# A conv, state-space and attention block: the scan's input in a ring of three PSUM banks, the depthwise 3x3 on shifted copies, and TensorE work in smaller pieces

## The chip, the cores and the metric

The kernel runs on one core of a Trainium2 chip. The metric is the device time of the whole program in microseconds (us). Profiles are of one execution, taken by the hardware profiler. The engines are called PE (TensorE, matrix multiplication), PEld (its weight loads), DVE (VectorE), ACT (ScalarE), POOL (GpSimd) and SP (SyncE, which issues the DMAs). PSUM is the memory that PE writes, eight banks of 128 partitions x 512 float32 values.

## The reference

Input x has 8 images of 384 channels and 32 x 32 pixels (1024 positions). Layer 0 adds to x a selective state-space model, run forward and backward over the positions, and a gated depthwise convolution. Layer 1 is causal attention with 6 heads, then a feed-forward network with weights that are Kronecker products. All is float32.

```python
# layer 0, per direction; xn = rmsnorm(x) over channels
u, z = split(in_proj(xn))
u = silu(causal_conv4(u) + conv1d_b)
dt, Bm, Cm = split(x_proj(u))
delta = softplus(dt_proj(dt) + dt_proj_b)
deltaA = exp(delta[..., None] * A)
deltaBu = (delta * u)[..., None] * Bm[:, :, None, :]
h[t] = deltaA[t] * h[t-1] + deltaBu[t]       # 16 states for each of 384 channels
y = (sum_n h[n] * C[n] + u * D) * silu(z)
global_feat = out_proj(y)                    # forward + backward, times scale_mod
local_feat = sigmoid(depthwise3x3(xn) + dw_b) * xn
x = x + res_scale * (global_feat + local_feat)
# layer 1, on tokens
t = t + attention(layernorm(t))
t = t + gelu(layernorm(t) @ kron(c_fc_1, c_fc_2).T) @ kron(c_proj_1, c_proj_2).T
```

## The kernel before

**One list of operations, ordered by a planner.** The program first declares every operation (`op`, lines 105 to 153) with its engine, an assumed cost, what it reads and writes, and a due time `at`. `Plan.run` (155 to 264) then goes through an assumed clock: each engine in turn takes, of the operations that could start now, the one with the earliest due time. The outcome is one fixed order for each engine, and the engines meet only through semaphores. An operation here may hold several instructions, which then stand together on the engine; a projection, for instance, is one operation of three matmuls. The assumed costs (`pe`, `act`, `dve`, `pool`, 79 to 92) shape the order only, they aren't waited for. A `Window` (407 to 424) spreads due times over a stretch, and `EVICT`, `SUMS`, `PRODUCTS`, `DECAY` (403) move due times of some kinds forward. `STAY` (98) is how long ACT prefers operations with the activation table that is loaded.

**Buffers** are slots of a kind (`kinds`, 379 to 383). The PSUM banks are divided into five for general use (`psm`), one pair for the scan's input (`b`), and one for the scan's output sums (`y`). Most tiles in the other memory share 26 slots (`t`).

**The scan** (`scans` 841, `group` 905). A group is 8 channels x 16 states on 128 partitions, over 1024 positions; there are 96 groups per image (48 in each direction), 768 in all. A group takes these steps: a DMA broadcasts delta to `dA`, with six slots (914); ACT makes exp(delta*A) of it (919); PE spreads delta*u to the 16 states with two matmuls, one per half of the positions, into `b` (926 to 931); DVE multiplies `b` by B, in place (932); DVE scans, reading `dA` and `b` (935); POOL multiplies by C (938); PE sums over the states into `y`, on four groups of 32 columns (875 to 884). The matmul for a group is declared to come as early as it can, but `b` has one slot, so it waits until the scan of the group before has read it.

**Around it** run, for other images, `project` (613, input projection), `gates` (681), `prepare` (692, the convolution of 4 taps, as four column groups on shifted copies, then `products` and `delta`), `local` (741, the depthwise 3x3 and its gate), `finish` (941) and `layer1` (1019, attention and the feed-forward network). `local` multiplies, for every block of 128 channels and half, nine diagonal 128 x 128 matrices by shifted views of the padded image `xm`, in three operations of three matmuls. `delta` (795) makes two matmuls of 24 rows, one for each half, in turn. In `project_in` DVE adds the bias of v when it takes v from PSUM (1062).

Matmuls all have line 311 in the profile, since a helper issues them; a row is told apart by its tiles (`pw` is the depthwise bank, `b` the scan's input, `s` the scores, `t` the transposes). A float32 matmul of the program is two instructions in the profile. DMAs all have line 391.

Of the kernel before, what the change touches and what calls it, by code (L numbers as in the profile page):

```python
# [9 lines left out]
F32 = mybir.dt.float32  # L10
# [7 lines left out]
P = 128  # L18
# [12 lines left out]
TAPS = 4  # L31
KP = 4
# [58 lines left out]
def pe(n, k=1):  # L91
    return k * (0.04 + n * 0.0012)


class Plan:
    LATENCY = 0.15
    SWITCH = 1.3
    STAY = 7.0
# [169 lines left out]
def conv_attn_hybrid_kernel(  # L268
# [85 lines left out]
    nc.vector.tensor_reduce(by4, ident.rearrange("p (m k) -> p m k", k=TAPS), AX.X, ALU.max)  # L354
    eye8 = const.tile([P, GC], F32, name="eye8")
# [12 lines left out]
    for c in range(CT):  # L368
# [8 lines left out]

    TB = PADDED * 4
# [3 lines left out]
        "psm": (5, HALF * 4), "b": (1, L * 4), "y": (1, HALF * 4),  # L382
    }
    sb = ctx.enter_context(tc.tile_pool(name="sb", bufs=1))
    pp = ctx.enter_context(tc.tile_pool(name="pp", bufs=1, space=PSUM))
    plan = Plan({k: n for k, (n, _) in kinds.items()})
# [11 lines left out]

    EXP, SILU, GELU = "natural_log_exp_and_others", "silu_and_others", "gelu_and_others"
# [3 lines left out]
    EVICT, SUMS, PRODUCTS, DECAY = 0.0, 10.0, 10.0, 15.0  # L403

    PREPARE, PROJECT, LAYER1 = (0.05, 0.75), (0.7, 1.0), (1.1, 2.1)
# [39 lines left out]
    wld = [array([P, 9, P], f"wld_{c}") for c in range(CT)]  # L445
# [6 lines left out]
    w_dt = held([P, P], "w_dt")  # L452
# [3 lines left out]
    bvb = held([P, C], "bvb")  # L456
# [4 lines left out]
    def setup_early():  # L461
# [52 lines left out]
        for c in range(CT):  # L514
            dma(
                lambda c=c: w_dt.t[c * KI : c * KI + RANK, :], lambda c=c: dt_wT[:, c * P : (c + 1) * P], [], [(w_dt, c)], 0
            )
# [22 lines left out]
    def setup_late():  # L540
# [5 lines left out]
        for c in range(CT):  # L546
            wl = tl(f"wlm_{c}", [P, 9, P])
            for k in range(9):
                op(
                    "POOL", 0.4, lambda wl=wl, c=c, k=k: nc.gpsimd.tensor_scalar_mul(wl.t[:, k], ident, col("dw_w", c, k)),  # L550
                    [], [(wl, k)],
                )
            dma(lambda c=c: wld[c].t, lambda wl=wl: wl.t, [wl], [wld[c]], P * 9 * P * 4)
# [7 lines left out]
    def setup_layer1():  # L561
# [6 lines left out]
        dma(lambda: bvb.t, lambda: bv.partition_broadcast(P), [], [bvb], 0)  # L568
# [44 lines left out]
    def project(b):  # L613
# [21 lines left out]
        for hf in range(NH):  # L635
            p = bank(f"pss_{b}_{hf}")

            def total(p=p, hf=hf):
                for c in range(CT):
                    mm(p.t, ones, sq[c].t[:, half(hf)], c == 0, c == CT - 1)  # L640

            op("PE", pe(HALF, 3), total, sq, [p], holds=xp)
# [15 lines left out]
    def into(b, w, xp, win):  # L658
# [3 lines left out]
        for m in range(CT):  # L662
            t = tl(f"{'uz'[w]}t_{b}_{m}")
            for hf in range(NH):
                p = bank(f"pi_{b}_{w}_{m}_{hf}")

                def proj(p=p, m=m, hf=hf):
                    for c in range(CT):
                        mm(grid(p.t), win.t[:, c, chans(m)], inside(xp[c].t, hf), c == 0, c == CT - 1)

                op("PE", pe(HALF, 3), proj, [(v, hf) for v in xp] + [win], [p], holds=[t])
                op("ACT", act(HALF), lambda p=p, t=t, hf=hf: nc.scalar.copy(t.t[:, half(hf)], p.t), [p], [(t, hf)])  # L672
# [19 lines left out]
    def prepare(b):  # L692
# [5 lines left out]
        for c in range(CT):  # L698
# [11 lines left out]
            for hf in range(NH):  # L710
                for d in range(2):
# [9 lines left out]
                    op("PE", pe(HALF, 2.4), conv, ct + [wc], [p], holds=[u])  # L721
# [19 lines left out]
    def local(b):  # L741

        s = b % 2
        for c in range(CT):
            xr, xm, wl = tl(f"xr_{b}_{c}"), tl(f"xm_{b}_{c}", [P, PADDED]), tl(f"wl_{b}_{c}", [P, 9, P])
            dma(lambda t=wl: t.t, lambda c=c: wld[c].t, [wld[c]], [wl], P * 9 * P * 4)
            dma(lambda t=xm: t.t, lambda c=c: xpd[s].t[chans(c)], [(xpd[s], c)], [xm], P * PADDED * 4)
            dma(lambda t=xr: t.t, lambda c=c: x[b, chans(c)].rearrange("p h w -> p (h w)"), [], [xr], P * L * 4)
            for hf in range(NH):
                p = bank(f"pw_{b}_{c}_{hf}")  # L750

                for dy in range(3):

                    def conv(p=p, hf=hf, wl=wl, xm=xm, dy=dy):
                        xg = xm.t.rearrange("p (h w) -> p h w", w=WP)
                        for dx in range(3):
                            mm(
                                grid(p.t), wl.t[:, dy * 3 + dx], xg[:, dy + hf * RH : dy + (hf + 1) * RH, dx : dx + W],
                                dy + dx == 0, dy + dx == 4,
                            )  # L760

                    op("PE", pe(HALF, 3), conv, [xm, wl], [p], holds=[xr])
# [7 lines left out]
                def mix(p=p, hf=hf, xr=xr, xm=xm):  # L770
                    nc.vector.scalar_tensor_tensor(grid(p.t), grid(p.t), 1.0, inside(xm.t, hf), ALU.add, ALU.mult)
                    nc.vector.scalar_tensor_tensor(
                        xr.t[:, half(hf)], p.t, hres.t, xr.t[:, half(hf)], ALU.mult, ALU.add
                    )

                op("DVE", 2 * dve(HALF), mix, [xm, hres], [p, (xr, hf)])
            dma(lambda c=c: based[s].t[chans(c)], lambda t=xr: t.t, [xr], [(based[s], c)], P * L * 4)

    def products(b, d, us, wc):
# [3 lines left out]
        for hf in range(NH):  # L783
            p = bank(f"px_{b}_{d}_{hf}")

            def proj(p=p, hf=hf):
                for c in range(CT):
                    mm(p.t, wc.t[:, c, 0:P], us[d][c].t[:, half(hf)], c == 0, c == CT - 1)

            op("PE", pe(HALF, 3), proj, us[d] + [wc], [p], holds=[xd])  # L790
# [4 lines left out]
    def delta(b, d, c, du, xd):  # L795
# [6 lines left out]
        r = slice(c * KI, c * KI + RANK)  # L802
        for hf in range(NH):
            p = bank(f"pd_{n}_{hf}")
            op(
                "PE", pe(HALF), lambda p=p, hf=hf: mm(p.t, w_dt.t[r, :], xd.t[r, half(hf)]),
                [(xd, hf), (w_dt, c)], [p], holds=[e, de],
            )

            def split(p=p, hf=hf):  # L810
# [3 lines left out]
            op("ACT", 2 * act(HALF) + 0.1, split, [p], [(e, hf), (de, hf)])  # L814
# [565 lines left out]
```

## Time and profile before

| | us |
|---|---|
| median of 3 runs (lowest, highest) | 4458.82 (4454.85, 4462.86) |
| the profiled execution | 4449.86 |
| its span, first to last instruction | 4448.1 |
| first scan starts | 151.5 |
| last scan starts | 4185.0 |

The page cuts the span into 40 slices; each digit is the busy share of a slice in tenths. The scans run from slice 2 to slice 38, and no engine is at 9 throughout:

```profile
PE   5587777789897998989997898979989798888798
DVE  1566768888788788788788787888878788888622
ACT  4648554676667657676577666677567665556355
POOL 2957846896469855797559964698548974576322
DMA  6786795577876669566776678667795667456300
```

A group of instructions is read as line, engine, operation, what it writes and reads, their sizes and the count, then busy us and mean ns of one, then the engine's idle time just before such instructions and which instruction ended most of it. The next rows are of other operations that the change touches:

```profile
L1316 ACT ACT_TABLE_LOAD x234 | 300.2, 1283 | 4.2
L311 PE MATMUL pd<-xd,w_dt 24*128 24x512 f32 x192 | 115.8, 712 | 21.8 <-ACT de L812 18.7 <-ACT p L1108 2.1 <-DVE xr L772 0.8
L1064 DVE TENSOR_TENSOR v<-pvv,bvb 128x512 f32<-128x512 f32 x48 | 32.6, 680 | 66.6 <-PE pvv L311 66.6
```

### The profile page before, as it was taken

What the parts mean: (1) busy time and instruction counts of PE and PEld (TensorE: products, weight loads), DVE (VectorE), ACT (ScalarE), POOL (GpSimd) and SP (SyncE); (2) the same over time, 40 slices, a digit from 0 to 9 for tenths busy, and PEclk for the clock granted to TensorE, in tenths of its full rate; (3) what the DMA queues carried; (4) which work ended last, traced back from release to release, by engine and by line L of the source; (5) the groups of instructions that cost most, each with busy time, mean ns of one, the idle gap of its engine ahead of it and who ended that gap; (6) DMA issues with size and microseconds to landing.
All of it is one profiled execution on the core that took longest, in us unless ns stands there. A gap on an engine that the chain in (4) does not pass through costs nothing. (4 is left out here: it accounts for less than half of the span.)

```text
span 4448.1 us, 52858 instructions
## 1 busy us (share of the span) xinstructions
PE 3800.7 (85%) x17682; PEld 1558.8 (35%) x17682; DVE 3341.6 (75%) x2940; ACT 2799.7 (63%) x4524; POOL 3010.2 (68%) x2385
## 2 busy tenths in 40 slices
PE   5587777789897998989997898979989798888798
PEld 2132222334233442433323342334424343343254
DVE  1566768888788788788788787888878788888622
ACT  4648554676667657676577666677567665556355
POOL 2957846896469855797559964698548974576322
PEclk7697787799998999889998999989998899999799
DMA  6786795577876669566776678667795667456300
GB/s 212 232 272 201 229 270 165 163 226 204 220 200 178 209 185 274 159 199 207 222 220 179 206 212 220 203 180 208 212 255 163 202 182 205 136 146 181 98 6 34
DMA packets 297068, 853.55 MB, mean 192 GB/s; under 512 B 33812, under 2 KB 87132, under 8 KB 296796
## 3 DMA queue, kind: packets, MB, share of 16 engines
q1 hardware_dynamic: 296796, 850.18, 66.3%
q8 instruction: 140, 2.29, 0.2%
q14 instruction: 132, 1.08, 0.1%
HBM read 677.25 MB, written 174.59 MB: 192 GB/s over the span
## 5 line engine op out<-in xcount | busy, mean ns | idle before, releaser
L938 POOL TENSOR_TENSOR h<-h,bc 128x1024 f32<-128x1024 f32 x768 | 1811.9, 2363 | 1047.6 <-DVE h L935 745.6
L935 DVE TENSOR_TENSOR_SCAN h<-dA,b 128x1024 f32<-128x1024 f32 x768 | 1755.5, 2286 | 96.7 <-ACT dA L919 19.7
L932 DVE TENSOR_TENSOR b<-b,bc 128x1024 f32<-128x1024 f32 x768 | 943.8, 1229 | 652.5 <-PE b L311 532.3
L919 ACT ACTIVATE dA<-dA,nA 128x1024 f32<-128x1024 f32 x768 | 870.2, 1147 | 338.4 <-DMA dA<-ded 317.2
L311 PE MATMUL b<-du,dup 32*128 32x512 bf16 x1536 | 328.4, 421 | 403.3 <-DVE h L935 356.6
L311 PE MATMUL y<-h,sel 128*32 128x512 f32 x3072 | 599.5, 690 | 46.1 <-POOL h L938 45.0
L311 PE MATMUL pw<-xm,wl 128*128 128x512 f32 x864 | 413.8, 619 | 7.8 <-ACT de L812 4.2
L1108 ACT ACTIVATE p<-s,mx 128x512 f32<-128x512 f32 (+3 forms) x576 | 328.9, 580 | 123.6 <-DVE mx L1102 120.7
L311 PEld LDWEIGHTS <-dup 32*128 32x128 bf16 x1536 | 75.5, 92 | 909.0 <-DVE h L935 597.4
L1153 POOL TENSOR_SCALAR p<-p,den 128x512 f32<-128x512 f32 (+3 forms) x576 | 329.3, 592 | 80.3 <-DVE den L1146 79.0
L1167 ACT COPY pT<-t 128x512 f32<-128x512 f32 (+3 forms) x576 | 253.8, 486 | 176.2 <-PE t L1160 169.4
L1160 PE MATMUL t<-ident,p 128*128 128x128 f32 x1728 | 297.2, 311 | 77.3 <-POOL p L1153 54.9
L1102 DVE TENSOR_REDUCE mx<-s 128x1 f32<-128x512 f32 (+3 forms) x576 | 286.3, 545 | 70.2 <-PE s L311 63.5
L1316 ACT ACT_TABLE_LOAD x234 | 300.2, 1283 | 4.2
L1160 PEld LDWEIGHTS t<-ident,p 128*128 128x128 f32 x1728 | 216.2, 157 | 223.8 <-POOL p L1153 129.8
L311 PE MATMUL s<-k,q 64*128 64x512 f32 (+3 forms) x1152 | 286.2, 565 | 4.6 <-ACT p L1108 3.4
L311 PE MATMUL pi<-xp,win 128*128 128x512 f32 x576 | 274.6, 618 | 11.9 <-ACT zt L672 10.4
L311 PE MATMUL pc<-pT,v 128*64 128x128 f32 x3456 | 248.8, 292 | 5.6 <-ACT pT L1167 5.6
L311 PEld LDWEIGHTS pc<-pT,v 128*64 128x64 f32 x3456 | 201.3, 145 | 89.0 <-issue 45.0
L311 PEld LDWEIGHTS pw<-xm,wl 128*128 128x128 f32 x864 | 158.2, 195 | 195.7 <-issue 184.5
L838 POOL TENSOR_TENSOR u<-u,part 128x1024 f32<-128x1024 f32 x96 | 205.3, 2138 | 18.0 <-ACT part L830 18.0
L830 ACT CAST part<-u 128x1024 bf16<-128x1024 f32 x144 | 150.5, 1045 | 94.3 <-POOL u L838 51.6
(169 smaller groups left out, 4766.1 us busy)
## 6 DMA issues: line engine op xcount, KB each, us to landing
dA<-ded SPq DMA_DIRECT2D x768, 512.0 KB
ct<-urd SPq DMA_DIRECT2D x96, 513.5 KB
du<-dusd SPq DMA_DIRECT2D x96, 512.0 KB
dusd<-part SPq DMA_DIRECT2D x288, 128.0 KB
ded<-de SPq DMA_DIRECT2D x48, 512.0 KB
uz<-uzd SPq DMA_DIRECT2D x48, 512.0 KB
bc<-bcd SPq DMA_DIRECT2D x32, 512.0 KB
xpd<-xp SPq DMA_DIRECT2D x24, 578.0 KB
```

Of the source, the lines that this page charges most:

```text
L311: nc.tensor.matmul(out_, lhsT=lhsT, rhs=rhs, start=first, stop=last)
L838: "POOL", pool(L), lambda part=part: nc.gpsimd.tensor_sub(du.t, du.t, part.t), [part], [du]
L919: "ACT", act(L) + 0.1, lambda: nc.scalar.activation(dA.t, dA.t, AF.Exp, scale=nA.t[:, g : g + 1]),
L932: op("DVE", 1.15, lambda: nc.vector.tensor_mul(t.t, t.t, bc.t[:, 0]), [(bc, 0)], [t], at=at)
L935: lambda: nc.vector.tensor_tensor_scan(h.t[:, rev], dA.t[:, rev], t.t[:, rev], 0.0, ALU.mult, ALU.add),
L938: op("POOL", pool(L), lambda: nc.gpsimd.tensor_mul(h.t, h.t, bc.t[:, 1]), [(bc, 1)], [h], at=at - PRODUCTS)
L1102: nc.vector.tensor_reduce(mx.t[:, g, hh : hh + 1], sc[hh].t[:, 0:w], AX.X, ALU.max, negate=True)
L1108: nc.scalar.activation(ps[hh].t[:, k0:k1], sc[hh].t[:, 0 : k1 - k0], AF.Exp, bias=mx.t[:, g, hh : hh + 1], accum_out=den.t[:, g, hh : hh + 1],
L1153: nc.gpsimd.tensor_scalar(t, t, den.t[:, g, hh : hh + 1], 1.0, ALU.mult, ALU.mult)
L1160: nc.tensor.transpose(t.t[:, j * P - k0 : (j + 1) * P - k0], ps[hh].t[:, j * P : (j + 1) * P], ident)
L1167: nc.scalar.copy(pT[hh].t[:, k0 // P : k1 // P, :].rearrange("p j t -> p (j t)"), t.t[:, 0 : k1 - k0])
L1316: nc.scalar.preload_act_table_set(table)
```

## The change

Eight things change together.

1. The scan's input gets three neighbouring banks, `ring`, in place of one pair. A group uses the middle bank and one outer bank, the left for one group and the right for the next. In the left case the outer bank holds the first half of the positions and the middle one the second; in the right case it is the other way round, so that a group's two banks always lie side by side in the order of the positions. Each half has its own matmul operation and its own product by B; the scan is one instruction as before.
2. The general banks become four.
3. The depthwise 3x3 works on copies of 32 channels x 3 horizontal shifts (96 partitions), loaded by DMA, with four groups of 32 columns: three steps (the vertical taps) of four matmuls. The weights are small blocks in place of diagonal matrices.
4. The two halves of `delta` become one operation on different rows of the array, into two banks.
5. Matmuls that accumulate become one operation each (`accumulate`); the operations for v, the context, the scores' maxima and exponentials, and the layer norm are cut likewise.
6. The bias of v is added where ACT takes the context from PSUM.
7. The planner's costs for PE are new: `pe`, `pair`, `quad`.
8. Due times and `STAY` are new.

```diff
 def pe(n, k=1):
-    return k * (0.04 + n * 0.0012)
+    return k * (0.02 + n * 0.00185)
+def pair(n):
+    return 0.1 + n * 0.0019
+def quad(n):
+    return 0.1 + n * 0.0019
...
-    STAY = 7.0
+    STAY = 15.0
...
-        "psm": (5, HALF * 4), "b": (1, L * 4), "y": (1, HALF * 4),
+        "psm": (4, HALF * 4), "bs": (2, HALF * 4), "bm": (1, HALF * 4), "y": (1, HALF * 4),
...
+    ring = pp.tile([P, 3 * HALF], F32, tag="ring", name="ring")
...
+    def accumulate(terms, p, cost, holds=(), **kw):
+        for i, (args, reads) in enumerate(terms):
+            first, last = i == 0, i == len(terms) - 1
+            def term(args=args, first=first, last=last):
+                mm(*args(), first, last)
+            op("PE", cost, term, reads, [p], holds=holds if first else (), **kw)
...
-    EVICT, SUMS, PRODUCTS, DECAY = 0.0, 10.0, 10.0, 15.0
-    PREPARE, PROJECT, LAYER1 = (0.05, 0.75), (0.7, 1.0), (1.1, 2.1)
+    EVICT, SUMS, PRODUCTS, DECAY = 20.0, 30.0, 10.0, 25.0
+    PREPARE, PROJECT, LAYER1 = (0.0, 0.7), (0.75, 1.0), (1.1, 2.0)
...
+            xs = []
+            for g in range(RG):
+                t = tl(f"xs_{b}_{c}_{g}", [DX * KI, PADDED])
+                a = xpd[s].t[c * P + g * KI : c * P + (g + 1) * KI, 0 : PADDED - DX + 1]
+                src = bass.AP(tensor=a.tensor, offset=a.offset, ap=[[PADDED, KI], [1, DX], [1, PADDED - DX + 1]])
...
-                for dy in range(3):
-                    def conv(p=p, hf=hf, wl=wl, xm=xm, dy=dy):
-                        xg = xm.t.rearrange("p (h w) -> p h w", w=WP)
-                        for dx in range(3):
+                for dy in range(DX):
+                    def conv(p=p, c=c, hf=hf, xs=xs, dy=dy):
+                        for g in range(RG):
+                            xg = xs[g].t.rearrange("p (h w) -> p h w", w=WP)
                             mm(
-                                grid(p.t), wl.t[:, dy * 3 + dx], xg[:, dy + hf * RH : dy + (hf + 1) * RH, dx : dx + W],
-                                dy + dx == 0, dy + dx == 4,
+                                grid(p.t[g * KI : (g + 1) * KI, :]), wl.t[:, c * RG + g, dy],
+                                xg[:, dy + hf * RH : dy + (hf + 1) * RH, 0:W], dy == 0, dy == DX - 1,
                             )
-                    op("PE", pe(HALF, 3), conv, [xm, wl], [p], holds=[xr])
+                    op("PE", quad(HALF), conv, xs + [wl], [p], holds=[xr])
...
+        ps = [bank(f"pd_{n}_{hf}") for hf in range(NH)]
+        def both():
+            for hf in range(NH):
+                r = slice((c + hf) % CT * KI, (c + hf) % CT * KI + RANK)
+                mm(ps[hf].t, w_dt[hf].t[r, :], xd.t[r, half(hf)])
+        op("PE", pair(HALF), both, [xd] + [(w, c) for w in w_dt], ps, holds=[e, de])
...
-        t = Val("b", [P, L], f"b_{n}")
-        def spread():
-            for hf in range(NH):
+        side, mid = Val("bs", None, f"bs_{n}"), Val("bm", None, f"bm_{n}")
+        def place(v):
+            hf = side.slot if v is side else 1 - side.slot
+            o = (side.slot + hf) * HALF
+            return hf, ring[:, o : o + HALF]
+        for v in (side, mid):
+            def spread(v=v):
+                hf, to = place(v)
                 rr = slice((r * NH + hf) * KI, (r * NH + hf + 1) * KI)
-                mm(t.t[:, half(hf)], dup[rr, :], du3.t[rr, j])
-        op("PE", 0.5, spread, [du3], [t], at=-1000.0 + at * 1e-3)
-        op("DVE", 1.15, lambda: nc.vector.tensor_mul(t.t, t.t, bc.t[:, 0]), [(bc, 0)], [t], at=at)
+                mm(to, dup[rr, :], du3.t[rr, j])
+            op("PE", 0.24, spread, [du3], [v], at=-1000.0 + at * 1e-3)
+        for v in (side, mid):
+            def times_b(v=v):
+                hf, to = place(v)
+                nc.vector.tensor_mul(to, to, bc.t[:, 0, half(hf)])
+            op("DVE", dve(HALF), times_b, [(bc, 0)], [v], at=at)
+        def scan():
+            t = ring[:, side.slot * HALF : side.slot * HALF + L]
+            nc.vector.tensor_tensor_scan(h.t[:, rev], dA.t[:, rev], t[:, rev], 0.0, ALU.mult, ALU.add)
+        op("DVE", 2.21, scan, [dA, side, mid], [h], at=at)
...
-                op("PE", pe(P, 12) + 0.5, proj_v, [(t, g) for t in xn] + [w], [p], holds=[v])
-                op(
-                    "DVE", dve(HALF),
...
+                    op("PE", pe(P, 3), proj_v, [(t, g) for t in xn] + [w], [p], holds=[v])
+                op("ACT", act(HALF), lambda p=p, v=v, g=g: nc.scalar.copy(v.t[:, half(g)], p.t), [p], [(v, g)])
```

## The prediction

> **What bounds the kernel now.** I read the page's busy times first, then its groups of instructions, then the waits, then the stretches, then one stretch of the timeline. All sums below are against the profiled execution (span 4448.1 us, time 4449.9 us); the median of the runs shown, 4458.8 us, is 9 us above it.
>
> Busy times (engine, busy us, share of the span, instructions):
> ```profile
> PE 3800.7 (85%) x17682; PEld 1558.8 (35%) x17682; DVE 3341.6 (75%) x2940; ACT 2799.7 (63%) x4524; POOL 3010.2 (68%) x2385
> ```
> No engine is full. PE is the busiest, DVE the next that could become the bound.
>
> Groups (busy us, mean ns of one, then idle of the engine before them and its releasers):
> ```profile
> L935 DVE TENSOR_TENSOR_SCAN h<-dA,b 128x1024 f32<-128x1024 f32 x768 | 1755.5, 2286 | 96.7 <-ACT dA L919 19.7
> L932 DVE TENSOR_TENSOR b<-b,bc 128x1024 f32<-128x1024 f32 x768 | 943.8, 1229 | 652.5 <-PE b L311 532.3
> ...
> L311 PE MATMUL b<-du,dup 32*128 32x512 bf16 x1536 | 328.4, 421 | 403.3 <-DVE h L935 356.6
> L311 PE MATMUL y<-h,sel 128*32 128x512 f32 x3072 | 599.5, 690 | 46.1 <-POOL h L938 45.0
> L311 PE MATMUL pw<-xm,wl 128*128 128x512 f32 x864 | 413.8, 619 | 7.8 <-ACT de L812 4.2
> ```
> DVE and PE wait for each other around the buffer b: the matmul that fills b waits for the scan that still reads it, and the product in b waits for the matmul.
>
> Waits (engine and line that waited, for whom: us in total, times, longest):
> ```profile
> DVE b L932 <- PE b L311: 532.3, 476, 7.9
> PE b L311 <- DVE h L935: 356.6, 236, 5.0
> ACT dA L919 <- DMA dA<-ded: 317.2, 154, 6.7
> ```
> Stretches: from the first scan to the last (150 to 4187), and the rest. Columns: us, busy us of PE, PEld, DVE, ACT, POOL, then PE clock, DMA share, GB/s.
> ```profile
> 150.00:4187.00 4037.00, 3474.62 (x16135) 1396.67 (x16134) 3253.16 (x2729) 2600.01 (x4100) 2890.39 (x2173) 0.91 0.70 202
> 4187.00:4448.00 261.00, 238.79 (x1303) 126.67 (x1302) 72.05 (x146) 120.00 (x327) 56.82 (x146) 0.95 0.08 28
> ```
> The scan stage is what the change can shorten. DVE is idle there for 4037 - 3253 = 784 us, of which 532 is the wait for b; no other releaser costs it over 33 us there (a wait of 104 us for pd ends with the first product and lies before the stage). The tail is the last image's layer 1, 239 of 261 us PE, and holds little of the changed work.
>
> Timeline of one step at its shortest (start, duration, instruction; idle before it in brackets):
> ```profile
> 2022.05 2.29 DVE L935 TENSOR_TENSOR_SCAN h<-dA,b 128x1024 f32<-128x1024 f32 x1
> ...
> 2024.39 0.39 PE L311 MATMUL b<-du,dup 32*128 32x512 bf16 x2
> ...
> 2024.82 1.23 DVE L932 TENSOR_TENSOR b<-b,bc 128x1024 f32<-128x1024 f32 x1 [0.49 <-PE b L311]
> ```
> Even with PE ready, DVE stands 0.49 us between scan and next product. The mean of the 476 waits is 532.3/476 = 1.12 us, so the rest, 0.63 us each, is PE arriving late from other work.
>
> **What the Trainium skill says.** "TensorE: Matmul & The Clock Gate", section "Part 3: Packing small matmuls — row/col tiling", says that matmuls on different column groups of the array run at the same time, about as long as one. The trace agrees: eight y instructions on four column groups took 1.07 us, six pw instructions on the full array 2.74. "Perfetto Trace Analysis", "Optimizing Scalar/DVE Operations", gives some 125 ns of fixed cost to each DVE instruction on PSUM; here two products of 512 (679 ns each, L771) against one of 1024 (1229) cost 129 ns more, which I use. The same page, "Matmul Optimizations", asks for all eight PSUM banks to be used; both kernels do, but divide them differently.
>
> **The change part by part.**
> Ring of three banks. Step n+1's outer half goes to the bank that scan n doesn't read, so its matmul needs no wait for scan n; only the middle half must wait. After scan n DVE multiplies the outer half (0.68 us), and in that time PE fills the middle (the 0.49 us above, or less with one matmul instead of two). A wait is thus hidden up to 0.68 us. I went through the waits for b in DVE's timeline and added up only what each has above 0.68: 245 us of 532 are left if PE is as late as now. PE will be less late (next two points), so I take 170. Bounds: 50, if PE is nearly always in time, and 350, if its order fits worse. The price: 768 x 0.13 us = 100 us more of DVE. In total -532 + 170 + 100 = -262. The middle half's matmul still waits for scan n, and PE works in order: behind it stands every later matmul, as today behind b (the 357 us above); 236 such waits, 1.5 us each, pass on to whoever needs PE next. With less to do PE may stand there longer, which costs nothing while DVE is at the scan.
>
> Depthwise 3x3. Three horizontal shifts lie in the partitions (96 of them), so per image, channel block and half there are three groups of four column matmuls instead of nine full ones: 48 x 3 = 144 groups at 1.07 us instead of 144 pieces at 2.68 (two or three such pieces in the chain took 2.58 to 2.77). PE saves 144 x 1.61 = 232 us. Nothing of this is taken off the end directly, since PE is idle anyway; it pays through less lateness. It adds 12 loads of 96 x 1154 x 4 bytes = 443 KB per image, 42.5 MB, and saves about 12 MB of weights: 853.6 to 884 MB. The DMA share of the scan stage would go from 0.70 to 0.70 x 884/853.6 x 4037/3718 = 0.79. The stretch 150 to 650 ran at 0.82 already, so it fits, with longer waits for dA: nothing to +60 us; I take nothing, since scans waited only 19.7 us for dA in all and its decay is now put 25 instead of 15 earlier. The loads stand in SP's queue ahead of dA loads; SP itself waited 1715 us for scans to free buffers, so some 70 more issues of half a us find room. They also take three more of the 26 shared slots per block; that can delay work of the other stages, not shown by the trace, from nothing to +50 us; nothing taken.
>
> Both halves of delta together. Two halves in turn took 2.34 us (four pd instructions in the chain); in two row groups they should take what a score pair took, 1.13. They now need both halves of xd and two banks at once. 48 x 1.21 = 58 us of PE. With the 232 PE has 3475 - 290 = 3185 us in the stage.
>
> Pieces of one matmul. Same instructions, cut so that the spread for b can slip in after at most about 1.1 us rather than 2.7. Gain contained in the 170. The planner's prices change too: it held 0.654 us for a 512 matmul (three: 1.96) where the chain shows 2.58 to 2.77 for three; now 0.967 each, 2.90 for three. Pairs and groups of four are now priced at 1.07, which the trace confirms. An order made with truer prices should meet fewer late partners.
>
> Bias of v moves to the copy of the context on ACT. DVE loses 42 additions of 0.68 in the stage, 29 us, and their waits for pvv, 28.6 us: -57. ACT gains 48 copies of 0.585 and about 0.1 us on 192 context copies, 47 us, inside its 37% of idle time. The longer stay with a table can save some of the 234 loads of 1.28 us; from nothing to -100 us on ACT, none on the path.
>
> Setup. 27 POOL products of 0.6 us become 12 smaller ones; nine element-wise loads are added. They aren't needed before the first scan at 151.5 us: nothing, or +-10.
>
> Banks. The rest of the program has four banks instead of five. PE hardly waits for evictions now (7.7 us for g, 8.1 for de, in the stage). Bounds 0 and +450, see the last rival; I take 0, because evictions now get 20 us of priority and the halves of a score are evicted singly.
>
> Sum: 4037 - 262 - 57 = 3718 for the scan stage; with 150 before, 261 after and 1.8 outside the span 4131 us. Check by engine: DVE 3253 + 100 - 29 = 3324 (89%), PE 3185 (86%), POOL unchanged 2890 (78%): no engine is overfull. Against the median this is 4140.
>
> **The rivals.**
> 1. DVE becomes the bound: of the wait for b only some 20 us and of the others 80 are left, 3324 + 100 = 3424, in all about 3840 to 3950. For it: PE loses 290 us. Against: both engines keep to one fixed order and meet 768 times.
> 2. The wait moves. The lost time returns as waits for dA loads, for shared slots or for banks: half the net gain, 4449.9 - 160 = 4290, up to 4440. For it: the 317 us of ACT waiting for dA and the higher DMA share.
> 3. The ring doesn't separate: if it is guarded as one buffer, the outer half's matmul still waits for the scan. Then +100 for two products, -57 for v, and a third of the lateness (476 x 0.63 = 300 us), -100: about 4390. The trace of before has no such buffer and can't decide it.
> 4. Slower: banks. I count 2304 uses of a bank in the program, some 2030 in the scan stage. Four banks over 4037 us give 4 x 4037/2030 = 7.9 us per use before the pace falls below today's, 7.3 at the forecast's. A full-width score pair held its two banks from 2027.17 to 2032.28, 5.1 us, a depthwise bank nearly 18 (2011.9 to 2029.75). If waits between matmul and eviction bring the mean over 7.9, banks set the pace; at 8.2, 8.2 x 2030/4 = 4160 us of stage, 4575 in all. Against: transposes hold a bank for under 2 us, and they are a quarter of the uses.
> 5. No change that can be told.
>
> **How the numbers follow.** Forecast 0.54 (own range 4010 to 4260); rival 1 0.13, rival 2 0.14, rival 3 0.05, rival 4 0.11, no change 0.03. About 0.2% (9 us) is what a measurement can tell. Faster: 0.54 + 0.13 + 0.14 + 0.05 = 0.86; same 0.03; slower 0.11. The range 3930 to 4400 leaves out rival 4, no change, a third of rival 1 and a little of rival 2.
>
> **What would show it.** Right: the wait of the products for PE falls from 532 to 100 to 250 us; two products of 512 about 0.65 to 0.7 us each; the depthwise row of PE near 150 us; PE busy 290 us lower; DVE at 80% of the span. Wrong: waits of PE for evictions (ACT p, ACT pT, DVE mx) of over 150 us would speak for banks; dA waits over 450 us for the loads; spreads of the outer half that begin only at the end of a scan for rival 3. What would make the forecast wrong is an order in which the outer half's matmul or product is placed too late, so that nothing lies between scan and middle half.

## The result, and the profile after

The changed kernel is slower: 4520.07 us (median; 4510.73 to 4526.95) against 4460.21 us (the kernel before, four runs), a ratio of 1.0134 with a 95% interval of 1.0113 to 1.0156. The forecast was 4140 us, so its direction failed and not only its size. The profiled execution has a span of 4524.9 us; its first scan starts at 153.4 and its last at 4239.3.

Busy times of the changed kernel, on the page (columns as before):

```profile
PE 3627.5 (80%) x17970; PEld 1498.8 (33%) x17970; DVE 3430.3 (76%) x3661; ACT 2887.0 (64%) x4598; POOL 2999.1 (66%) x2370
```

PE has 173 us less to do than before, and the program takes longer. So something else in the change costs more than this work was worth.

Groups of the changed kernel:

```profile
L1008 DVE TENSOR_TENSOR_SCAN h<-dA,ring 128x1024 f32<-128x1024 f32 x768 | 1755.5, 2286 | 276.5 <-PE y L321 136.9
L1002 DVE TENSOR_TENSOR ring<-ring,bc 128x512 f32<-128x512 f32 x1536 | 1070.8, 697 | 448.9 <-PE ring L321 424.4
...
L321 PE MATMUL ring<-du,dup 32*128 32x512 bf16 x1536 | 333.5, 412 | 684.7 <-DVE ring L1002 483.2
...
L321 PE MATMUL y<-h,sel 128*32 128x512 f32 x3072 | 521.6, 675 | 17.9 <-POOL h L1011 17.4
```

The third row is the one to look at. Before, PE waited 357 us for scans before it filled `b`. Now it waits 483 us for *products*, L1002. No value that this matmul reads or overwrites comes from a product that ended so late; the timeline below shows which product it is.

Waits of the changed kernel (engine and line that waited, for whom: us in total, times, longest):

```profile
PE ring L321 <- DVE ring L1002: 483.2, 415, 5.0
DVE ring L1002 <- PE ring L321: 424.4, 493, 112.4
ACT dA L976 <- DMA dA<-ded: 183.2, 107, 5.6
...
PE ring L321 <- DVE h L1008: 172.4, 175, 7.6
...
DVE h L1008 <- PE y L321: 136.9, 43, 8.7
```

PE stands before the ring for 483 + 172 = 655 us in place of 357. The wait of DVE fell only to 424 us, 112 of them before the first product of the program, so some 311 in the scan stage where it was 532. New is the last line: scans wait 137 us in all for a free `h`, which the sums `y` on PE release (3 us before).

Two steps of the changed kernel, DVE timeline (start, duration, instruction; idle before it):

```profile
1737.24 2.29 DVE L1008 TENSOR_TENSOR_SCAN h<-dA,ring 128x1024 f32<-128x1024 f32 x1
...
1741.57 2.29 DVE L1008 TENSOR_TENSOR_SCAN h<-dA,ring 128x1024 f32<-128x1024 f32 x1
1743.89 0.70 DVE L1002 TENSOR_TENSOR ring<-ring,bc 128x512 f32<-128x512 f32 x1
1745.08 0.70 DVE L1002 TENSOR_TENSOR ring<-ring,bc 128x512 f32<-128x512 f32 x1 [0.48 <-PE ring L321]
1745.91 2.29 DVE L1008 TENSOR_TENSOR_SCAN h<-dA,ring 128x1024 f32<-128x1024 f32 x1
```

And PE beside it:

```profile
1740.31 0.39 PE L321 MATMUL ring<-du,dup 32*128 32x512 bf16 x2 [1.03 <-DVE ring L1002]
...
1744.65 0.39 PE L321 MATMUL ring<-du,dup 32*128 32x512 bf16 x2 [1.19 <-DVE ring L1002]
```

The scan ends at 1743.86 and the outer half's product follows at 1743.89, as the forecast had it: its matmul was early. But the middle half's matmul doesn't start at 1743.9, when the scan has left its bank. It starts at 1744.65, which is 0.06 us after the *outer* product ended (1744.59), though that one works in another bank. So the 0.48 us stand between the two products in place of before the one, and one step takes 1741.57 - 1737.24 = 4.33 us. Over the DVE timeline the median of steps with nothing but scan and products is 4.34 us (386 steps); before it was 4.36 (292 steps).

Over the whole run the outer half's matmul began before the end of the scan of the step before in all 767 steps that have one. The middle half's began within 0.1 us after the end of the outer product in 418 of them, and within 0.1 us after the end of the scan in 216. The trace names the semaphore that it waited for, which the scan and the products raise alike, but not the count. One guard of the tile `ring` as a whole explains this: the middle matmul then waits for the last product or scan before it in the program's order, whichever bank that was in. The first experiment tests it. Of the 768 middle matmuls only 103 tell their completion themselves; for the others it is told with that of the next outer one behind, which is the second of the x2 above.

Stretches of the changed kernel: the scan stage and the rest (columns as before):

```profile
153.00:4241.00 4088.00, 3282.68 (x16383) 1330.64 (x16382) 3340.79 (x3449) 2670.48 (x4153) 2882.38 (x2166) 0.90 0.72 206
4241.00:4525.00 284.00, 258.04 (x1338) 133.76 (x1338) 72.13 (x145) 131.43 (x341) 56.55 (x146) 0.98 0.09 31
```

The stage is 51 us longer and PE in it 192 us less busy; the rest is 23 us longer.

### The profile page after: what moved, and what is told of

The parts are those of the page before. It is cut to its first block, busy times and chain, and to the rows that moved or that the text cites. A ratio compares the mean times of both kernels' runs of the same rounds, so it can differ in the third digit from the quotient of the medians.

```text
span 4524.9 us, 54500 instructions
## 1 busy us (share of the span) xinstructions
PE 3627.5 (80%) x17970; PEld 1498.8 (33%) x17970; DVE 3430.3 (76%) x3661; ACT 2887.0 (64%) x4598; POOL 2999.1 (66%) x2370
## 2 busy tenths in 40 slices
DMA packets 308914, 884.12 MB, mean 195 GB/s; under 512 B 39080, under 2 KB 92344, under 8 KB 308632
## 4 chain that ended last, share of the span: by engine, by line
DVE 47%; PE 28%; POOL 7%; ACT 7%; issue 6%; DMA 4%; SPq 1%; DVEq 0%; POOLq 0%; ACTq 0%
DVE h L1008 26%; DVE ring L1002 15%; PE ring L321 5%; PE pc L321 4%; POOL h L1011 3%; DVE mx L1170 3%; PE y L321 2%; PE t L1230 2%; PE pq L321 2%; PE s L321 2%; PE px L321 1%; DMA dA<-ded 1%; ACT L1407 1%; PE pg L321 1%; ACT dA L976 1%
## 5 line engine op out<-in xcount | busy, mean ns | idle before, releaser
L1008 DVE TENSOR_TENSOR_SCAN h<-dA,ring 128x1024 f32<-128x1024 f32 x768 | 1755.5, 2286 | 276.5 <-PE y L321 136.9
L1002 DVE TENSOR_TENSOR ring<-ring,bc 128x512 f32<-128x512 f32 x1536 | 1070.8, 697 | 448.9 <-PE ring L321 424.4
L321 PE MATMUL ring<-du,dup 32*128 32x512 bf16 x1536 | 333.5, 412 | 684.7 <-DVE ring L1002 483.2
L321 PE MATMUL y<-h,sel 128*32 128x512 f32 x3072 | 521.6, 675 | 17.9 <-POOL h L1011 17.4
L321 PEld LDWEIGHTS <-dup 32*128 32x128 bf16 x1536 | 125.0, 92 | 1156.1 <-issue 1143.5
L321 PE MATMUL s<-k,q 64*128 64x512 f32 (+3 forms) x1152 | 301.8, 568 | 23.4 <-ACT p L1177 19.7
L321 PE MATMUL pi<-xp,win 128*128 128x512 f32 x576 | 294.5, 626 | 9.6 <-ACT zt L709 9.1
L321 PE MATMUL pc<-pT,v 128*64 128x128 f32 x3456 | 276.9, 304 | 2.9 <-ACT pT L1237 2.4
L321 PEld LDWEIGHTS y<-h,sel 128*32 128x32 f32 x3072 | 78.8, 113 | 256.9 <-issue 124.5
L1262 ACT ACTIVATE cT<-pc,bvc 128x128 f32<-128x128 f32 x192 | 70.3, 366 | 146.2 <-PE pc L321 144.6
```

The source lines that it names most:

```text
L321: nc.tensor.matmul(out_, lhsT=lhsT, rhs=rhs, start=first, stop=last)
L1002: nc.vector.tensor_mul(to, to, bc.t[:, 0, half(hf)])
L1008: nc.vector.tensor_tensor_scan(h.t[:, rev], dA.t[:, rev], t[:, rev], 0.0, ALU.mult, ALU.add)
```

## The experiments

All times are medians, and ratios are to the kernel before on the same chip, with 95% intervals. Two theories stood at first: that the guard of the ring as one buffer costs the time, or that the order, the banks and the due times do.

**The guard taken away.** Waits between PE and DVE are dropped where their instructions touch different banks of the ring; all that touch the same bank are kept.

```diff
+    touched = []
+    def apart(i, banks):
+        for o, theirs in touched:
+            if not banks & theirs and o.ins.engine != i.ins.engine:
+                tc.declare_no_dep(i.ins, o.ins, reason="other bank of the ring")
+        touched.append((i, banks))
...
-                mm(to, dup[rr, :], du3.t[rr, j])
+                apart(nc.tensor.matmul(to, lhsT=dup[rr, :], rhs=du3.t[rr, j], start=True, stop=True), banks)
```

> The changed kernel, with the semaphore waits between matmuls and DVE instructions on different banks of the ring taken out; order on every engine as in the changed kernel. Theory A (the ring is guarded as one buffer: the middle half's matmul waits for the outer half's product, so the gap of 0.48 us per step stays, and the second product of a step costs 0.13 us more on top): the waits of the second product fall from about 240 us to under 60, PE's waits for the ring's products from 483 to near nothing, and the time falls by 150 to 350 us, to 4170 to 4370. Theory B (the order, four banks and new due times cost the time; the guard costs little): 4470 to 4520, and the waits move to scans and evictions.

Measured: 4379.92 us, 0.9832 (0.9815 to 0.9849), with the order of the changed kernel; 10 us slower than the range of theory A and far from theory B. The guard alone costs 4520 - 4380 = 140 us. In that is also that nearly every middle matmul, 755 of 768, now tells its completion itself. The scan of one step and the matmul for the next (the middle half, with the outer one behind it):

```profile
1963.38 2.28 DVE L1018 TENSOR_TENSOR_SCAN h<-dA,ring 128x1024 f32<-128x1024 f32 x1
...
1965.71 0.39 PE L1005 MATMUL ring<-du,dup 32*128 32x512 bf16 x2 [0.55 <-DVE h L1018]
```

The matmul starts 0.05 us after the scan's end, without the outer product between. So it is in 564 steps (within 0.1 us), and in 5 only it follows the outer product. Waits of this run:

```profile
PE ring L1005 <- DVE h L1018: 460.4, 452, 7.6
...
DVE ring L1012 <- PE ring L1005: 222.2, 129, 107.3
```

PE no longer waits for products: scans are nearly all it waits for at the ring. DVE has 222 - 107 = 115 us of waiting in the stage. Steps with nothing else took 4.03 us (median of 386).

**The pair back.** All of the change but the ring: `b` of two banks, one product of 1024, five general banks.

```diff
-        "psm": (4, HALF * 4), "bs": (2, HALF * 4), "bm": (1, HALF * 4), "y": (1, HALF * 4),
+        "psm": (5, HALF * 4), "b": (1, L * 4), "y": (1, HALF * 4),
```

> The changed kernel with the pair of banks of the kernel before, one product of 1024 per step, and five general banks; all else as changed. Theory A: the ring as guarded only cost, so this is faster than the changed kernel by about its products (768 x 0.13 = 100 us) and by the waits that the guard added at the scans: 4330 to 4420, faster than before by 1 to 3%. Theory B: it stays at 4460 to 4520, since order and due times are kept.

Measured: 4308.64 us, 0.9672 (0.9655 to 0.9689), faster even than theory A. Without the ring the change is a gain. The ring, with the bank that it takes from the others, costs even when it isn't guarded as one: 4380 against 4309.

**Ring alone, depthwise alone,** each put into the kernel before with its order, prices and due times; the ring here without the needless waits. (Diffs: point 1 with the edit above, and point 3, of the change.)

> The kernel before with the ring alone, waits between different banks taken out, and four general banks; depthwise, pieces, planner's costs and due times as before. Theory A: most of the 532 us of waits for b go, 100 us of products come: 4150 to 4330. Theory B: four banks with the order of before cost as much as the ring brings: 4400 to 4520.

> The kernel before with the depthwise 3x3 on shifted copies alone. PE loses about 230 us of work. If PE's lateness at b is what costs (theory A of the prediction) it brings 50 to 120 us: 4340 to 4410. If the floor of 0.49 us per step and the fixed order hold the time, 4430 to 4470.

Measured: ring 4514.74 us, 1.0135 (1.0117 to 1.0153), in theory B's range; depthwise 4470.4 us, 1.0041 (1.0023 to 1.0059), at the upper edge of its second range. With the ring alone, against the kernel before, products wait 305 us less for PE in the stage, but DVE works 213 us longer there, its other waits grow by 120, and 42 us more lie after the last scan. Theory B's reason, four banks in the order of before, wasn't tried by itself. Busy times with the depthwise alone:

```profile
PE 3682.0 (82%) x17970; PEld 1459.7 (33%) x17970; DVE 3339.2 (75%) x2941; ACT 2774.2 (62%) x4506; POOL 2997.5 (67%) x2370
```

PE loses 119 us of work and the program gains nothing; the products' wait for PE in the stage goes from 548 to 519 us only. In the order of before, less work for PE hardly brings it to the products earlier.

**What in the ring costs.** Three runs on top of the pair: one general bank fewer; the product in two halves; the ring without needless waits, but with one product over both banks.

```diff
-        "psm": (5, HALF * 4), "b": (1, L * 4), "y": (1, HALF * 4),
+        "psm": (4, HALF * 4), "b": (1, L * 4), "y": (1, HALF * 4),
```

> The changed kernel with the pair of banks b and one product of 1024 (as in e2_pair), but four general banks in place of five; one bank stays unused. Theory A (what the ring costs beyond its guard, the 71 us between e1_apart 4380 and e2_pair 4309, is the two products of 512): four banks cost next to nothing, 4300 to 4325. Theory B (the fifth bank given up is what costs): 4345 to 4400, with PE's waits for evictions (ACT p, ACT pT, DVE mx) over 60 us higher than in e2_pair.

```diff
-        op("DVE", 1.15, lambda: nc.vector.tensor_mul(t.t, t.t, bc.t[:, 0]), [(bc, 0)], [t], at=at)
+        for hf in range(NH):
+            op("DVE", dve(HALF),
+                lambda hf=hf: nc.vector.tensor_mul(t.t[:, half(hf)], t.t[:, half(hf)], bc.t[:, 0, half(hf)]),
+                [(bc, 0)], [(t, hf)], at=at)
```

> e2_pair with the product by B done as two instructions of 512 one after the other, pair b and five banks kept. From before, e1_apart and e3_ring_alone I read 0.28 us more from the start of the first product to the start of the scan with two products (1.34 to 1.62); 768 x 0.28 = 215 us of DVE. Theory A (the split is the price of the ring): DVE busy 100 to 130 us higher, its idle before the second product small but present, and the time 4440 to 4530, since here nothing is won back by an earlier matmul. Theory B (the split is cheap, the banks or the order cost): below 4400.

```diff
+        def times_b():
+            t = ring[:, side.slot * HALF : side.slot * HALF + L]
+            apart(nc.vector.tensor_mul(t, t, bc.t[:, 0]), {side.slot, side.slot + 1})
+        op("DVE", 1.15, times_b, [(bc, 0)], [side, mid], at=at)
```

> e1_apart (ring, engines wait for each other only where they touch the same bank, four general banks) with one product of 1024 over both banks in place of two of 512. Only the middle half's matmul then stands between scan and product. Theory A (the split product is what makes e1_apart slower than the pair; an early outer half is worth something by itself): DVE busy 100 to 125 us lower than e1_apart, the bare step 4.15 to 4.25 us, between e5_pair_4banks's 4.36 and e1_apart's 4.03; time 4240 to 4300. Theory B (what makes e1_apart slower is its wait of scans for a free h, 128 us, which comes from the order and stays): 4310 to 4390.

Measured: four banks 4303.63 us, 0.9646 (0.9628 to 0.9665), so giving up the fifth bank costs nothing that can be told here (theory A). Split product 4361.58 us, 0.9782 (0.9767 to 0.9796): 53 us, which is theory B's range: part of the 0.2 us a step is paid out of waits that shrink. As banks and split bring no more than some 50 of the 76 us between the ring without guard and the pair with four banks, something else comes with the ring. Ring with one product 4361.17 us, 0.9792 (0.9751 to 0.9833).

Two steps with the split product on the pair, DVE timeline:

```profile
1783.17 1.43 DVE L992 TENSOR_TENSOR b<-b,bc 128x512 f32<-128x512 f32 x2 [0.49 <-PE b L321]
1784.74 2.29 DVE L997 TENSOR_TENSOR_SCAN h<-dA,b 128x1024 f32<-128x1024 f32 x1
1787.51 1.43 DVE L992 TENSOR_TENSOR b<-b,bc 128x512 f32<-128x512 f32 x2 [0.48 <-PE b L321]
1789.07 2.29 DVE L997 TENSOR_TENSOR_SCAN h<-dA,b 128x1024 f32<-128x1024 f32 x1
```

From the start of the first product to that of the scan it is 1.57 us here; with one product of 1024 it was 1.34 (median) in the kernel before.

The stages, from DVE's timelines (us; the stage from the first scan's start to the last one's end; idle is what the timeline lists before instructions, and working is the rest, gaps too short for the list included):

| run | stage | working | idle | of it: products for PE | scans |
|---|---|---|---|---|---|
| before | 4036 | 3326 | 710 | 548 | 27 |
| after | 4088 | 3438 | 650 | 311 | 207 |
| guard away | 3949 | 3516 | 433 | 115 | 194 |
| pair, four banks | 3880 | 3299 | 581 | 408 | 90 |
| pair, product split | 3939 | 3443 | 496 | 364 | 59 |
| ring, one product | 3896 | 3297 | 598 | 366 | 98 |

With the guard away the ring saves 408 - 115 = 293 us of waiting for PE against the pair with four banks. It pays 3516 - 3299 = 217 us for the second product (0.28 us a step) and 104 us more of scans that wait; other waits take 41 more. Net the stage is 69 us longer. Why the sums release `h` late with two products on the ring I haven't settled. With one product the scans wait only 98 us, so the 4361 lies in theory B's range but not for its reason. The middle matmul and the wait for it stand again behind the scan, the stage is no shorter than the pair's, and some 34 of the 54 us by which this run's span exceeds that of the pair with four banks lie after the last scan.

**Prices, due times and pieces.** The pair with the planner's numbers of before, in three ways: the price of one matmul and the due times, the price alone, the due times alone (`STAY` goes with the due times).

```diff
-    return k * (0.02 + n * 0.00185)
+    return k * (0.04 + n * 0.0012)
...
-    STAY = 15.0
+    STAY = 7.0
...
-    EVICT, SUMS, PRODUCTS, DECAY = 20.0, 30.0, 10.0, 25.0
+    EVICT, SUMS, PRODUCTS, DECAY = 0.0, 10.0, 10.0, 15.0
...
-    PREPARE, PROJECT, LAYER1 = (0.0, 0.7), (0.75, 1.0), (1.1, 2.0)
+    PREPARE, PROJECT, LAYER1 = (0.05, 0.75), (0.7, 1.0), (1.1, 2.1)
```

> e2_pair with the planner's price for a matmul, its stay with a table and its due times as in the kernel before. Theory A (the new prices and due times bring most of what e2_pair gains, 148 us, since depthwise alone brought nothing): 4410 to 4480. Theory B (the gain comes from the work itself, pieces of one matmul, halves of delta together, bias of v): 4300 to 4350.

> e2_pair with the old price for one matmul of 512 (0.65 in place of 0.97 us), but the new stay and due times. Theory A (the truer price makes the better order): 4430 to 4490, as e7_pair_old_times. Theory B (the earlier due times for evictions, sums and decays make it): 4290 to 4350.

> e2_pair with the new price for a matmul but the stay and due times of the kernel before: the fourth corner beside e7_pair_old_times (old, old: 4485), e11_pair_old_price (old price, new due times: 4540) and e2_pair (new, new: 4309). Theory A (the price alone carries the gain): 4280 to 4350. Theory B (price and due times are needed together): 4380 to 4470.

| us (ratio, 95% interval) | old price, 0.65 us | new price, 0.97 us |
|---|---|---|
| old due times | 4485.27 (1.0048 to 1.0083) | 4350.37 (0.9721 to 0.9781) |
| new due times | 4539.52 (1.0174 to 1.0221) | 4308.64 (0.9655 to 0.9689) |

The price carries most of it: 135 us with the old due times, 231 with the new. The due times give 42 us with the new price and cost 54 with the old. All three runs came out above their theory A: the first by 5 us, the old price alone by 50, the old due times alone by 0.4; none came to its theory B. Each corner is one fixed order, and only two prices were tried. That the price pays because it is nearer to the trace, and not because this one order happens to fit, is argued, not shown. The product by B of the pair (new, new), from the groups:

```profile
L989 DVE TENSOR_TENSOR b<-b,bc 128x1024 f32<-128x1024 f32 x768 | 944.2, 1229 | 523.6 <-PE b L321 511.7
```

and with the old price:

```profile
L989 DVE TENSOR_TENSOR b<-b,bc 128x1024 f32<-128x1024 f32 x768 | 943.9, 1229 | 687.6 <-PE b L321 678.9
```

The product takes the same time, only PE is later: 167 us of the difference stand in this one wait. The share of full TensorE clock that the profile shows as granted differs too: 0.87 in the profiled runs with the old price, 0.89 with the new. With the old due times PE is busy as long at both prices (3655 and 3659 us), so slower matmuls don't account for those 135 us. With the new due times it is busy 3728 us at the old price and 3634 at the new, and how much of the 231 us comes of that isn't separated.

The same numbers in the kernel before, whose pieces are of three matmuls; and the pair with the depthwise of before, nine full matmuls a bank, but in pieces of one:

```diff
-                    op("PE", pe(HALF, 3), conv, [xm, wl], [p], holds=[xr])
+                accumulate([(lambda p=p, hf=hf, wl=wl, xm=xm, k=k: tap(p, hf, wl, xm, k // 3, k % 3), [xm, wl])
+                    for k in range(9)], p, pe(HALF), [xr])
```

> The kernel before with nothing of the change but the planner's prices for PE, its stay with a table and its due times. e7_pair_old_times showed that e2_pair without the new numbers gains nothing. Theory A (the numbers alone bring the gain and the smaller pieces only let it in or not at all): 4290 to 4350. Theory B (the numbers pay only with work in pieces of one matmul, since only then the planner can use them): 4400 to 4470.

> e2_pair with the depthwise 3x3 of the kernel before (nine full-width matmuls a bank on the padded image, no shifted copies), but in pieces of one matmul at the new price. PE gets 140 to 230 us of work more than in e2_pair. Theory A (in an order that fits, PE's load doesn't set the end either, as e4_depthwise_alone said of the order of before; pieces with true prices are the whole gain): 4290 to 4340. Theory B (once the order fits, PE's load is felt, and the shifted copies bring part of the gain): 4360 to 4460.

Measured: numbers alone 4500.42 us, 1.0104 (1.0084 to 1.0124), no gain and even above theory B; full depthwise 4359.99 us, 0.9786 (0.977 to 0.9803), at the lower edge of theory B. The new numbers paid only together with the small pieces, and then without the shifted copies too. Busy times of the last run:

```profile
PE 3814.8 (88%) x17682; PEld 1529.0 (35%) x17682; DVE 3313.5 (76%) x2892; ACT 2848.5 (65%) x4568; POOL 3015.7 (69%) x2385
```

PE is busier than in the kernel before (3800.7) and the program 2.1% faster. On top of that order the shifted copies give 4360 - 4309 = 51 us.

**A buffer freed by the product.** To free the pair `b` earlier, the product was written to `h`, and the scan then worked in `h` in place.

```diff
-        op("DVE", 1.15, lambda: nc.vector.tensor_mul(t.t, t.t, bc.t[:, 0]), [(bc, 0)], [t], at=at)
+        op("DVE", 1.15, lambda: nc.vector.tensor_mul(h.t, t.t, bc.t[:, 0]), [t, (bc, 0)], [h], at=at)
```

> e2_pair with the product by B written to h, in which the scan then works in place, so that the pair b is free after the product and not after the scan. The next group's matmuls can then run during the scan. If the 0.49 us between scan and next product is what a bare step costs, and the product stays at 1.23 us, bare steps fall from 4.31 to about 3.85: some 365 x 0.45 = 160 us less, and the wait of the products for PE b falls from 404 us to below 150: 4140 to 4220. Rival: the product or the scan is slower with its input in SBUF, or the product now waits for h (six slots, freed by the sums) instead of for PE: 4290 to 4380.

Measured: 5191.74 us, 1.1645 (1.1628 to 1.1662), a miss of the kind that the rival named, but far larger; the last section says what the trace shows.

## Why the prediction was wrong

**Ring, -262: the step that failed.** "Step n+1's outer half goes to the bank that scan n doesn't read, so its matmul needs no wait for scan n" held in all 767 steps. The next sentence, "in that time PE fills the middle", didn't: PE was made to wait until the outer product had ended. From the pair with four banks to the ring as changed it is 4304 to 4520, +216 us in place of -262. Rival 3, with a chance of 0.05, named the cause, a ring guarded as one buffer, but not the place: it had the outer half's matmul wait for the scan, which happened in none of 767 steps. Its 4390 us were wrong too: it put the guard's own cost at nothing and still let a third of the lateness go, where the guard cost 140 us. With the guard PE stands 655 us at the ring for products and scans, without it 460, and every matmul behind comes later. "The Trainium skill", page "PSUM — Partial Sum Buffer", section "PSUM bank collisions raise a hardware error", asks to guard PSUM by bank and quadrant, by bank in its simple form. The waits show a coarser guard here, over three banks, and the run without it shows that the finer one is worth 140 us.

**Two products, +100: mis-sized.** The 0.13 us came from means of single instructions. With two of 697 ns the busy time rose by 768 x (2 x 0.697 - 1.229) = 127 us. What counts in the step is the distance from the first product to the scan: some 0.28 us more with the guard away, 217 us in the stage. So even with the waits for PE at 115 us, better than the 170 forecast, the ring lost. Waits of scans, 104 us more and most of it for a free `h`, weren't in the sum at all.

**Depthwise, PE -232: right in size, wrong in what it pays.** Its rows add up to 171.4 us, from 413.8: -242. PE's total fell by 173 us only, not by the 290 forecast, since other rows grew (`ph` and `pc` by 28 us each, `pq` by 25, `pi` by 20). Bytes (884.12 MB) came out as forecast; the DMA share of 0.72 is that of 0.79 over the longer stage. The wait of ACT for dA fell from 317 to 183 us. But "it pays through less lateness" failed in the order of before (+0.4%); in the better order it pays 51 us.

**Halves of delta together, PE -58:** the row fell from 115.8 to 69.5 us, -46. **Bias of v, DVE -29 in the stage:** the work of DVE with the pair is 27 us less than before, right. Its wait of 66.6 us went along to ACT (`v` now waits 66.6 us for pvv). **ACT, +47:** it was +87; the table loads went from 234 to 260, which is 33 us, where I had expected fewer. **Setup, 0:** the first scan starts at 153.4 in place of 151.5 us, right.

**Pieces of one matmul and prices, "contained in the 170": mis-sized, and the largest part of what the change does well.** With the due times, delta and the bias of v they bring 4455 - 4360 = 95 us without ring and shifted copies. Neither brings it alone: new prices and due times on large pieces gave +1.0%, small pieces at the old price and due times, with the shifted copies, +0.65%. That delta and the bias have a share in the 95 us isn't excluded; neither was tried by itself.

**Banks, 0: right.** Four in place of five are 5 us apart, inside the intervals. Rival 4 foresaw the sign and not the cause: PE and its weight loads waited 19.7 and 61.8 us for ACT's `p` before the scores, together well under the 150 us that it named.

The whole, from run to run: 4457 - 95 (pieces, prices, due times, delta, bias) - 51 (shifted copies) - 5 (bank) + 76 (ring with its own costs) + 140 (its guard) = 4522, against 4520 measured. It closes because each run differs from the next by one of these steps; in another order the steps would have other sizes, as those taken alone show. The fastest version is the change without the ring: 4304 us with four banks, 3.5% under the kernel before.

## What to carry to other kernels

A buffer that is split into banks is only as separate as the semaphores around it: look in the timeline whether the early instruction starts when its own bank is free, before counting on the overlap. Where a fixed order is planned from assumed costs, check the price of the commonest piece against the trace and make pieces small enough that the order can use it; here the new price was worth 135 us or more with small pieces and, with new due times, nothing with large ones, and 242 us of removed matrix work 51 at best. Price a split of an instruction by the distance between its neighbours in the timeline, not by the sum of the parts.

## What the runs showed of the hardware

I hadn't expected that the scan would lose so much with both its inputs outside PSUM. Groups of the run with the product in `h`:

```profile
L995 POOL TENSOR_TENSOR h<-h,bc 128x1024 f32<-128x1024 f32 x768 | 2145.3, 2803 | 816.5 <-DVE h L992 689.0
L992 DVE TENSOR_TENSOR_SCAN h<-dA,h 128x1024 f32<-128x1024 f32 x768 | 2387.7, 3113 | 81.7 <-ACT dA L975 34.7
```

In the pair these means are 2361 and 2285 ns, with the same shapes. The timeline of that run, DVE and POOL together:

```profile
2008.31 2.34 DVE L992 TENSOR_TENSOR_SCAN h<-dA,h 128x1024 f32<-128x1024 f32 x1
...
2010.82 2.35 POOL L995 TENSOR_TENSOR h<-h,bc 128x1024 f32<-128x1024 f32 x1 [2.32 <-PE pi L321]
...
2011.80 3.53 DVE L992 TENSOR_TENSOR_SCAN h<-dA,h 128x1024 f32<-128x1024 f32 x1
...
2015.50 2.36 POOL L995 TENSOR_TENSOR h<-h,bc 128x1024 f32<-128x1024 f32 x1 [2.32 <-PE ph L321]
```

The scan that starts at 2011.80 while POOL multiplies ends at 2015.33, which is 2.16 us after POOL's end at 2013.17: it did its work after POOL, not beside it. The next product of POOL begins 0.17 us after the scan. Over the whole run 656 scans began while POOL worked, and nine in ten of them ended between 2.14 and 2.17 us after POOL's instruction, however long that still had to run; the 80 with no POOL instruction beside them took 2.28 us. "The Trainium skill", page "SBUF — State Buffer", section "SBUF: two separate sides", says that a VectorE instruction with two SBUF inputs and a GpSimd instruction that reads SBUF take one shared pair of ports in turn, each for its whole length. The run agrees. With one input in PSUM, as in the other kernels here, scans took 2285 to 2286 ns on average, and in the pair those 624 that began while POOL worked took no longer than the others. The edit as a whole costs 5192 - 4309 = 883 us. DVE's scans are busy 633 us longer and POOL's products 335. It has a second price, which the rival had named too: the product needs a free `h`, and waits 245 us for the sums on PE to release one. How the 883 us divide between the two isn't separated.
